# A scan's main loop: from a scheduler's order to a fixed source order, a tile of the next group's projections around each step of the mixing

## The chip, the cores and the metric

The kernel runs on one core of a Trainium2 chip, in one launch. The metric is the device time of one execution in microseconds (us). Five engines have a queue of instructions each and work through it in order: TensorE (PE: matmuls, with the loading of weights shown apart as PEld), VectorE (DVE), ScalarE (ACT), GpSimd (POOL) and SyncE (SP, which issues the DMA transfers). An instruction that waits for another engine holds up all that stand behind it in its own queue.

## The reference

The kernel computes a layer of three parts, each added to `x` (16 x 32 x 512): a graph attention over a context, a state-space scan, and a small gated feed-forward network. The change touches the scan alone. Cut to what matters (128 heads of 64 channels, 8 groups of 16 heads, 128 states; sequences of 32, so one chunk holds a whole sequence):

```python
proj = jnp.einsum('bsd,od->bso', h, in_proj_w)
gate = proj[..., :D_INNER]                       # D_INNER = 8192
hBC = jax.nn.silu(causal_conv(hBC, conv_w, conv_b))
hid, B, C = split(hBC)
dt = jax.nn.softplus(dt + dt_bias)
A = -jnp.exp(A_log)
L = jnp.exp(segsum(A * dt))                      # decay from one position to a later one
M = einsum('bcihn,bcjhn->bcijh', C, B) * L
y = einsum('bcijh,bcjhp->bcihp', M, hid * dt) + Dp * hid
yg = y * jax.nn.silu(gate)
ygr = yg * rsqrt(mean over a group of 1024 channels of yg**2 + EPS)
out = residual + (ygr * gnorm_w) @ out_proj_w.T
```

## The kernel before

The graph part takes the first 1300 us and more, the scan runs until 2276 us of the profiled execution, and the feed-forward part follows. All 512 tokens are four blocks of 128. In the scan, tokens lie along the free axis wherever channels lie on the partitions. The 8192 inner channels are 64 tiles of 128 channels, two heads each; eight tiles make a group.

Per tile `t` (group `g`, step `i`) the work is:

- `project` (L1177): the weights of a tile (256 KB, `win`, a ring of six buffers shared by the gate half `wing` and the current half `winch`) are loaded by SP (L1174) and four matmuls of 128x512 make a product in PSUM (`pp`, two buffers). For the gate half ACT makes `gs = silu(pp)` (L1256).
- `convolve` (L1184 to L1192): for the current half, ACT writes the product times the last tap plus bias (`cy`), DVE adds the three other taps (L1189, three instructions), ACT makes `hid = silu(cy)` (L1192).
- `mix`, once for each tile of a group: four transposes of `hid` on PE (`pht`, L1285), DVE multiplies by `dt` (`hd`, L1287), DVE multiplies decay by `CB` for either head (`el`, L1298, two instructions), eight matmuls give the tile's output in PSUM (`py`, L1306). DVE adds `Dp * hid` (L1310) and multiplies by the gate (`gs`, L1311). ACT squares (L1316), POOL adds the square to the group's sum `ssq` (L1317; the first tile's square is written to `ssq` by ACT, L1313), and ACT scales by `gnorm_w` (L1318).
- `decays`, once for a pair of tiles (four heads): POOL makes `da` (L1265), one 128x512 matmul makes its running sums (`pl`, L1270), ACT takes the exponential (`ed`, L1275). `da` and `ed` have two buffers each. `pl` and `pht` share two PSUM buffers (`ps_m`).
- `close`, once for a group: four small matmuls sum `ssq` over the channels (`pn`, L1325), DVE and ACT make the inverse root (`rstd`, seven instructions), SP loads the eight tiles of the output weights (`wo`, 256 KB each, a ring of ten, L1333), and for each of the four token blocks eight 128x512 matmuls (`po`, L1338, two PSUM buffers) are added to `xt` by DVE, times the root (L1341).

The source runs `inner(g + 1)` (all eight tiles' projections and convolutions of the next group), then `mix(g)`, then `close(g)`. But that isn't the order of the queues: in the scan a scheduler orders instructions by priority and by when their inputs and buffers come free, so that on PE the projections, transposes, `py`, `pl` and `po` of two groups stand mixed, `py` matmuls partly one by one between others. On POOL it puts `da` as early as a buffer is free.

`inner` also advances `parts` by one step for each tile from the second group on. `parts` is the loading of the feed-forward part's low-rank weights (`LowRank.load`): ten pieces, each with nine small loads on SP (L185) and eight DVE instructions (`split`, L167 to L173).

Of the kernel before, what the change touches and what calls it, by code (L numbers as in the profile page):

```python
# [8 lines left out]
F32 = mybir.dt.float32  # L9
# [3 lines left out]
AF = mybir.ActivationFunctionType  # L13
ALU = mybir.AluOpType
# [4 lines left out]
P = 128  # L19
B = 16  # L20
C = 32
D = 512
# [9 lines left out]
CB = 3  # L32
# [8 lines left out]
H_M, G_M, SEQ = 128, 8, 32  # L41
D_INNER = 8192
NT = D_INNER // P
TG = NT // G_M
# [9 lines left out]
def kernel(ctx: ExitStack, tc: tile.TileContext, I, out):  # L54
# [69 lines left out]
    with ExitStack() as cx:  # L124
        scan_part(nc, tc, cx, I, id32, ones, xt, U, rstd, lows)
# [4 lines left out]
class LowRank:  # L130
# [4 lines left out]
    def __init__(self, nc, tc, const, I):  # L135
        self.nc, self.tc, self.I = nc, tc, I
        self.weights = {
            n: const.tile([P, w], BF16, name=f"lb{n}") for n, w in (("1", HT * NHT), ("3", HT * NHT), ("2", D))
        }
        self.values = {n: const.tile([P, D], BF16, name=f"lv{n}") for n in ("1", "3", "2")}  # L140

        self.of = [const.tile([LR, 3], F32, name=f"lof{k}") for k in range(2)]
# [969 lines left out]
def scan_part(nc, tc, cx, I, id32, ones, xt, u, rstd, lows):  # L1112
# [3 lines left out]
    wk = cx.enter_context(tc.tile_pool(name="swk", bufs=2))  # L1116
    sm = cx.enter_context(tc.tile_pool(name="ssm", bufs=3))
    wpool = cx.enter_context(tc.tile_pool(name="sw", bufs=4))
    ps_p = cx.enter_context(tc.tile_pool(name="sps_p", bufs=2, space=PSUM))
    ps_m = cx.enter_context(tc.tile_pool(name="sps_m", bufs=2, space=PSUM))  # L1120
    ps_y = cx.enter_context(tc.tile_pool(name="sps_y", bufs=2, space=PSUM))
# [24 lines left out]
    for t, base, cmul, op, b2, c2, s2 in ((le, 0, -1, ALU.is_ge, 0, 1, -32), (gt, 0, 1, ALU.is_gt, 31, -1, 32)):  # L1146
        nc.gpsimd.memset(t, 1.0)
        nc.gpsimd.affine_select(
            out=t, in_=t, compare_op=op, fill=0.0, base=base, pattern=[[-cmul, P]], channel_multiplier=cmul
        )  # L1150
        nc.gpsimd.affine_select(
            out=t, in_=t, compare_op=ALU.is_ge, fill=0.0, base=b2, pattern=[[s2, 4], [0, 32]], channel_multiplier=c2
# [10 lines left out]
    for q in range(4):  # L1163
        pt = ps_m.tile([P, 4, P], F32, tag="m", name=f"pt{q}")
# [6 lines left out]
    def project(t, tag):  # L1171

        w = wpool.tile([P, 4, P], F32, tag="win", name=f"win{tag}", bufs=6)
        nc.sync.dma_start(out=w, in_=I["in_proj"][t])  # L1174
        pp = ps_p.tile([P, D], F32, tag="p", name=f"pp{tag}")
        for k in range(4):
            nc.tensor.matmul(pp, lhsT=w[:, k], rhs=hT[:, k], start=(k == 0), stop=(k == 3))  # L1177
        return pp

    def convolve(dst, t, tag):  # L1180

        pp = project(NT + t, f"c{tag}")
        y = wk.tile([P, B, SEQ], F32, tag="cy", name=f"cy{tag}", bufs=3)
        nc.scalar.activation(  # L1184
            y.rearrange("p b s -> p (b s)"), pp, AF.Identity, bias=cb[:, t:t + 1], scale=cw[:, t, 3:4]
        )
        pv = pp.rearrange("p (b s) -> p b s", b=B)
        for sh in (1, 2, 3):
            nc.vector.scalar_tensor_tensor(  # L1189
                y[:, :, sh:], pv[:, :, :SEQ - sh], cw[:, t, 3 - sh:4 - sh], y[:, :, sh:], ALU.mult, ALU.add  # L1190
            )
        nc.scalar.activation(dst, y.rearrange("p b s -> p (b s)"), AF.Silu)  # L1192


    wdt = wpool.tile([P, 4, P], F32, tag="win", name="wdt", bufs=6)
# [36 lines left out]
    CB = sc.tile([P, G_M, 4, P], F32, name="CB")  # L1232
# [13 lines left out]
    parts = lows.load(low)  # L1246
    big = cx.enter_context(tc.tile_pool(name="sbig", bufs=2))

    def inner(g):

        gs = big.tile([P, TG, D], F32, tag="gs", name=f"gs{g}")
        hid = big.tile([P, TG, D], F32, tag="hid", name=f"hid{g}")
        for i in range(TG):
            t = g * TG + i
            pg = project(t, f"g{t}")
            nc.scalar.activation(gs[:, i], pg, AF.Silu)  # L1256
            convolve(hid[:, i], t, f"h{t}")
            if g > 0:
                next(parts, None)
        return gs, hid  # L1260

    def decays(h):

        da = sm.tile([P, 4, 4, SEQ], F32, tag="da", name=f"da{h}", bufs=2)
        nc.gpsimd.tensor_tensor(  # L1265
            da, lei.unsqueeze(1).unsqueeze(1).to_broadcast([P, 4, 4, SEQ]),
            dA[:, :, h:h + 4].rearrange("p q h -> p h q").unsqueeze(3).to_broadcast([P, 4, 4, SEQ]), ALU.mult,
        )
        pl = ps_m.tile([P, 4, 4, SEQ], F32, tag="m", name=f"pl{h}")
        nc.tensor.matmul(  # L1270
            pl.rearrange("p h q i -> p (h q i)"), lhsT=gt, rhs=da.rearrange("p h q i -> p (h q i)"),
            start=True, stop=True,
        )
        ed = sm.tile([P, 4, 4, SEQ], F32, tag="ed", name=f"ed{h}", bufs=2)
        nc.scalar.activation(ed, pl, AF.Exp)  # L1275
        return ed

    def mix(g, gs, hid):

        ssq = wk.tile([P, D], F32, tag="ssq", name=f"ssq{g}")  # L1280
        for i in range(TG):
            t = g * TG + i
            pt = ps_m.tile([P, 4, P], F32, tag="m", name=f"pht{t}")
            for q in range(4):
                nc.tensor.transpose(pt[:, q], hid[:, i, q * P:(q + 1) * P], id32)  # L1285
            hd = sm.tile([P, 4, 2, 64], F32, tag="hd", name=f"hd{t}")
            nc.vector.tensor_tensor(  # L1287
                hd, pt.rearrange("p q (h c) -> p q h c", h=2),
                dt[:, :, 2 * t:2 * t + 2].unsqueeze(3).to_broadcast([P, 4, 2, 64]), ALU.mult,
            )  # L1290
            py = ps_y.tile([P, 4, P], F32, tag="y", name=f"py{t}")
            if i % 2 == 0:
                decay = decays(2 * t)
            els = []
            for j in range(2):

                el = sm.tile([P, 4, P], F32, tag="el", name=f"el{2 * t + j}")
                nc.vector.tensor_tensor(  # L1298
                    el.rearrange("p q (b i) -> p q b i", b=4),
                    decay[:, 2 * (i % 2) + j].unsqueeze(2).to_broadcast([P, 4, 4, SEQ]),  # L1300
                    CB[:, g].rearrange("p q (b i) -> p q b i", b=4), ALU.mult,
                )
                els.append(el)
            for q in range(4):
                for j in range(2):
                    nc.tensor.matmul(  # L1306
                        py[64 * j:64 * j + 64, q], lhsT=hd[:, q, j], rhs=els[j][:, q], start=True, stop=True
                    )
            pyf = py.rearrange("p q t -> p (q t)")
            nc.vector.scalar_tensor_tensor(hid[:, i], hid[:, i], dpc[:, t:t + 1], pyf, ALU.mult, ALU.add)  # L1310
            nc.vector.tensor_tensor(gs[:, i], gs[:, i], hid[:, i], ALU.mult)  # L1311
            if i == 0:
                nc.scalar.activation(ssq, gs[:, i], AF.Square)  # L1313
            else:
                sq = wk.tile([P, D], F32, tag="sq", name=f"sq{t}")
                nc.scalar.activation(sq, gs[:, i], AF.Square)  # L1316
                nc.gpsimd.tensor_tensor(ssq, ssq, sq, ALU.add)  # L1317
            nc.scalar.activation(gs[:, i], gs[:, i], AF.Copy, scale=gnw[:, t:t + 1])  # L1318
        return ssq

    def close(g, gs, ssq):

        pn = ps_y.tile([P, 4], F32, tag="y", name=f"pn{g}")
        for q in range(4):
            nc.tensor.matmul(pn[:, q:q + 1], lhsT=ssq[:, q * P:(q + 1) * P], rhs=ones[:, 0:1], start=True, stop=True)  # L1325
        mean = sm.tile([P, 4], F32, tag="gm", name=f"gm{g}")
        nc.vector.tensor_scalar(mean, pn, 1.0 / (TG * P), None, ALU.mult)
        rs = sm.tile([P, 4], F32, tag="gr", name=f"gr{g}")
        rstd(sm, rs, mean, 4, f"gn{g}")
        wo = []  # L1330
        for i in range(TG):
            w = wpool.tile([P, D], F32, tag="wo", name=f"wo{g}_{i}", bufs=TG + 2)
            nc.sync.dma_start(out=w, in_=I["out_proj"][g * TG + i])  # L1333
            wo.append(w)
        for q in range(4):
            po = ps_o.tile([P, D], F32, tag="o", name=f"po{g}_{q}")
            for i in range(TG):
                nc.tensor.matmul(  # L1338
                    po, lhsT=gs[:, i, q * P:(q + 1) * P], rhs=wo[i], start=(i == 0), stop=(i == TG - 1)
                )  # L1340
            nc.vector.scalar_tensor_tensor(xt[:, q], po, rs[:, q:q + 1], xt[:, q], ALU.mult, ALU.add)  # L1341

    cur = inner(0)
    for g in range(G_M):
        nxt = inner(g + 1) if g + 1 < G_M else None
        ssq = mix(g, *cur)
        close(g, cur[0], ssq)
        cur = nxt


def ffn_part(nc, tc, cx, I, id32, xt, layernorm, lows, out):
# [139 lines left out]
```

## Time and profile before

| what | us |
|---|---|
| median of 3 runs | 2381.26 (2378.29 to 2382.47) |
| the profiled execution's own time | 2376.64 |
| its span in the profile | 2374.9 |
| first gate projection of the scan's loop starts | 1424.3 |
| last `po` matmul of the loop ends, about | 2275.7 |
| PE busy over the span | 2172.0 (91%) |
| DVE, ACT, POOL busy over the span | 1694.5, 1093.6, 831.4 |

The profile comes from one execution. Its page cuts the span into 40 slices of 59.4 us; the scan's loop lies in slices 25 to 39. The groups of instructions carry the source line, the engine, the operation and the tile that they write and read, then how many there were, their busy time and mean duration, and what the engine waited for before them. A 128x512 matmul in f32 appears as two records. Matmuls overlap: a record lasts 0.59 us, but the next may start 0.43 us after it, so costs on PE are read from start to start. The granted clock of PE is given per stretch: 1.00 is full speed.

### The profile page before, as it was taken

How to read it: one execution, taken by the hardware profiler on the slowest of the kernel's cores; microseconds unless marked ns; L12 is line 12 of the kernel's file. 1: busy time of each engine (PE TensorE's matmuls, PEld its weight loads, DVE VectorE, ACT ScalarE, POOL GpSimd, SP SyncE). 2: the span in 40 equal slices, each digit the busy share in tenths (PEclk: the TensorE clock that was granted, in tenths of full speed). 3: DMA queues.
4: the chain of work that ended last, by engine and by line, in shares of the span. 5: the costliest groups of instructions: out<-in, count | busy, mean ns of one | idle time of the engine just before them, and what ended most of it. 6: DMA issues, size and time to landing. Idle time of an engine off the chain costs nothing. (4 is left out here: it accounts for less than half of the span.)

```text
span 2374.9 us, 88834 instructions
## 1 busy us (share of the span) xinstructions
PE 2172.0 (91%) x39234; PEld 1243.6 (52%) x39234; DVE 1694.5 (71%) x3674; ACT 1093.6 (46%) x2023; POOL 831.4 (35%) x897
## 2 busy tenths in 40 slices
PE   5598899999989988799999689999999999999979
PEld 2254555776547765477777444444444444444422
DVE  8487897998979999799899757455362635446543
ACT  6685666556755544355555233233242423333321
POOL 2155656556555566555555100021120202012200
PEclk9899999999999999999999799999999999999989
DMA  1323242231231412313111212212212031220000
GB/s 49 81 59 76 51 81 57 52 81 43 59 78 42 90 41 55 81 43 85 43 39 41 94 56 79 72 53 58 67 40 84 23 102 49 63 62 14 27 36 18
DMA packets 121625, 137.99 MB, mean 58 GB/s; under 512 B 18398, under 2 KB 79506, under 8 KB 121154
## 3 DMA queue, kind: packets, MB, share of 16 engines
q1 hardware_dynamic: 121240, 132.32, 22.6%
q8 instruction: 308, 5.05, 0.9%
q14 instruction: 77, 0.63, 0.1%
HBM read 77.02 MB, written 12.85 MB: 38 GB/s over the span
## 5 line engine op out<-in xcount | busy, mean ns | idle before, releaser
L888 POOL TENSOR_TENSOR EN<-e,rz 128x480 f32<-128x480 f32 x344 | 342.4, 995 | 509.6 <-DVE rz L886 423.1
L913 PE MATMUL u<-WA,DD 128*32 128x128 bf16 (+1 forms) x16512 | 412.5, 248 | 19.4 <-issue 19.1
L918 ACT COPY us<-u 128x512 f32<-128x512 f32 x516 | 301.9, 586 | 154.2 <-PE u L913 138.2
L913 PEld LDWEIGHTS <-DD 128*32 128x32 f16 x16512 | 337.5, 97 | 53.5 <-issue 51.1
L873 ACT ACTIVATE e<-s,smc 128x480 f32<-128x480 f32 x344 | 227.3, 661 | 270.2 <-PE s L868 243.5
L809 POOL TENSOR_TENSOR DD<-fs,crep 128x480 f16<-128x480 f32 (+2 forms) x344 | 349.4, 1016 | 0.0
L941 PE MATMUL h<-e,us 128*32 128x30 f32 (+1 forms) x11008 | 281.3, 210 | 47.1 <-DVE e L894 25.6
L941 PEld LDWEIGHTS h<-e,us 128*32 128x32 f32 (+1 forms) x11008 | 247.2, 125 | 147.0 <-issue 68.1
L1189 DVE SCALAR_TENSOR_TENSOR cyh<-ppch,t_conv_w,cyh 128x496 f32<-128x496 f32 (+2 forms) x192 | 137.5, 716 | 221.9 <-ACT cyh L1184 217.9
L860 DVE TENSOR_REDUCE c<-s 128x16 bf16<-128x480 f32 x344 | 220.0, 640 | 77.0 <-PE s L851 73.9
L1265 POOL TENSOR_TENSOR da<-lei,dA 128x512 f32<-128x512 f32 x32 | 40.6, 1269 | 612.6 <-PE pl L1270 577.6
L1338 PE MATMUL po<-wo,gs 128*128 128x512 f32 x512 | 240.5, 605 | 10.4 <-DVE xt L1341 10.3
L1177 PE MATMUL ppch<-hT,winch 128*128 128x512 f32 x512 | 232.2, 593 | 0.0
L1177 PE MATMUL ppg<-hT,wing 128*128 128x512 f32 x512 | 231.9, 593 | 0.0
L894 DVE STREAM_TRANSPOSE e<-EN 128x512 f32<-128x512 f32 x344 | 224.5, 653 | 0.0
L880 DVE TENSOR_REDUCE z<-e 128x16 f32<-128x480 f32 x344 | 219.4, 638 | 0.4 <-ACT e L873 0.4
L541 ACT ACTIVATE sgn<-kd 128x512 bf16<-128x512 f32 x256 | 153.1, 598 | 48.6 <-PE kd L540 45.7
L851 PEld LDWEIGHTS <-DD 128*32 128x32 f16 x5504 | 80.8, 96 | 156.8 <-issue 131.6
L751 DVE TENSOR_SCALAR oh<-it,rank 128x512 bf16<-128x512 f16 x512 | 156.6, 366 | 7.6 <-PE pp L705 7.5
L1177 PEld LDWEIGHTS ppch<-hT,winch 128*128 128x128 f32 x512 | 93.6, 190 | 122.7 <-issue 122.4
L851 PE MATMUL s<-DX,DD 128*32 128x120 f16 x5504 | 141.5, 222 | 16.9 <-DMA DX<-DD 15.7
L1177 PEld LDWEIGHTS ppg<-hT,wing 128*128 128x128 f32 x512 | 95.8, 190 | 114.0 <-issue 114.0
(327 smaller groups left out, 2845.5 us busy)
## 6 DMA issues: line engine op xcount, KB each, us to landing
DX<-DD SPq DMA_DIRECT2D x456, 90.0 KB
wo<-in_out_proj SPq DMA_DIRECT2D x64, 256.0 KB
wing<-in_in_proj SPq DMA_DIRECT2D x64, 256.0 KB
winch<-in_in_proj SPq DMA_DIRECT2D x64, 256.0 KB
crep<-dC SPq DMA_DIRECT2D x128, 64.0 KB
dS<-so SPq DMA_DIRECT2D x32, 256.0 KB
fs<-dS SPq DMA_DIRECT2D x128, 64.0 KB
wincB<-in_in_proj SPq DMA_DIRECT2D x8, 256.0 KB
```

The source lines that it names most:

```text
L809: nc.gpsimd.tensor_tensor(d[:, :, m0 - n0:n1 - n0], win, crep[:, :, m0:n1].unsqueeze(3).to_broadcast([P, 4, n1 - m0, K]), ALU.subtract,)
L851: nc.tensor.matmul(s[rh, j * 4 * QB:(j + 1) * 4 * QB].rearrange("p (b q) -> p b q", b=4), lhsT=d[:, h, c0:c0 + 32], rhs=dx[:, h, :, c0:c0 ...
L860: nc.vector.tensor_reduce(c, live["s", at, gi].rearrange("p (i q) -> p i q", q=QB), AX.X, ALU.max, negate=True)
L873: nc.scalar.activation(e, s.rearrange("p (i q) -> p i q", q=QB), AF.Exp, scale=smc)
L880: nc.vector.tensor_reduce(z, e, AX.X, ALU.add)
L888: nc.gpsimd.tensor_tensor(en[:, :, :QB], e, rz.unsqueeze(2).to_broadcast([P, NI, QB]), ALU.mult)
L894: nc.vector.transpose(e.rearrange("p i q -> p (i q)"), en.rearrange("p i q -> p (i q)"))
L913: nc.tensor.matmul(u[rh, jj], lhsT=d[:, h, c0:c0 + 32], rhs=WA[k][:, h].rearrange("p b o -> p (b o)"), start=(jj == 0 and k == 0), stop=(k ...
L918: nc.scalar.copy(us[:, j - jj:j + 1], u)
L941: nc.tensor.matmul(h[r:r + co, pr, q0:q0 + QB], lhsT=us[:, j, b * co:(b + 1) * co], rhs=e[:, 4 * j + b, :QB], start=npair > 1, stop=True, ...
L1177: nc.tensor.matmul(pp, lhsT=w[:, k], rhs=hT[:, k], start=(k == 0), stop=(k == 3))
L1338: nc.tensor.matmul(po, lhsT=gs[:, i, q * P:(q + 1) * P], rhs=wo[i], start=(i == 0), stop=(i == TG - 1))
```

## The change

Around the whole loop the scheduler is turned off (`manual_schedule`): every queue now holds its instructions in the order in which the source issues them. The source is reordered with it.

- The first group's projections and convolutions are issued tile by tile ahead of the loop, and the first pair's decays.
- In step `i` of group `g` the source issues: the gate projection of tile `i` of the next group with its Silu on ACT; the end of the convolution of the tile before (three DVE instructions, Silu); `gated(i - 1)` (DVE twice, square on ACT, `ssq` add on POOL, scaling on ACT); `turn(i)` (transposes; in odd steps the decays of the next pair: `da` on POOL, `pl` on PE, `ed` on ACT; then `hd` and both `el` on DVE, and the load of this tile's `wo`); the current projection of the next group's tile with the first ACT instruction of its convolution; `outputs(i)` (the eight `py` matmuls).
- After the eighth step the convolution ends, `gated(7)` follows, and the group is closed with 32 `po` matmuls in one piece, `pn` and the root after the first eight.
- The closing of the seventh group is spread over the steps of the eighth, which has no projections of a next group: four `po` matmuls a step.
- `parts` advances at the end of each convolution.
- The `hd` ring goes from three buffers to two (`el` keeps three, `ed` and `da` two).

The instructions themselves are the same. The diff, cut to its core:

```diff
-    def inner(g):
...
+    cx.enter_context(tc.manual_schedule())
+    made = {}
+
+    def gate(g, i):
+        if i == 0:
+            made[g] = [big.tile([P, TG, D], F32, tag=n, name=f"{n}{g}") for n in ("gs", "hid")]
+        pg = project(g * TG + i, f"g{g * TG + i}")
+        nc.scalar.activation(made[g][0][:, i], pg, AF.Silu)
+
+    def current(g, i):
+        t = g * TG + i
+        yield from convolve_steps(made[g][1][:, i], t, f"h{t}")
+        if g > 0:
+            next(parts, None)
...
+    def ahead(h):
+        if h < H_M:
+            decay[h] = decays(h)
...
+        def turn(self, i):
...
             for q in range(4):
-                nc.tensor.transpose(pt[:, q], hid[:, i, q * P:(q + 1) * P], id32)
-            hd = sm.tile([P, 4, 2, 64], F32, tag="hd", name=f"hd{t}")
+                nc.tensor.transpose(pt[:, q], self.hid[:, i, q * P:(q + 1) * P], id32)
+            if i % 2:
+                ahead(2 * t + 2)
+            hd = sm.tile([P, 4, 2, 64], F32, tag="hd", name=f"hd{t}", bufs=2)
...
-            py = ps_y.tile([P, 4, P], F32, tag="y", name=f"py{t}")
-            if i % 2 == 0:
-                decay = decays(2 * t)
...
+            w = wpool.tile([P, D], F32, tag="wo", name=f"wo{t}", bufs=TG + 2)
+            nc.sync.dma_start(out=w, in_=I["out_proj"][t])
+            self.wo.append(w)
...
+        def gated(self, i):
...
                 nc.scalar.activation(sq, gs[:, i], AF.Square)
                 nc.gpsimd.tensor_tensor(ssq, ssq, sq, ALU.add)
             nc.scalar.activation(gs[:, i], gs[:, i], AF.Copy, scale=gnw[:, t:t + 1])
...
-    cur = inner(0)
+    for i in range(TG):
+        gate(0, i)
+        end_of(current(0, i))
+    ahead(0)
+    last = None
     for g in range(G_M):
-        nxt = inner(g + 1) if g + 1 < G_M else None
-        ssq = mix(g, *cur)
-        close(g, cur[0], ssq)
-        cur = nxt
+        mix = Mix(g)
+        conv = None
+        for i in range(TG):
+            if g + 1 < G_M:
+                gate(g + 1, i)
+            end_of(conv)
+            conv = None
+            if i:
+                mix.gated(i - 1)
+            mix.turn(i)
+            if g + 1 < G_M:
+                conv = current(g + 1, i)
+                next(conv)
+            else:
+                next(last, None)
+            mix.outputs(i)
+        end_of(conv)
+        mix.gated(TG - 1)
+        end_of(last)
+        last = mix.closing()
+        if g + 2 != G_M:
+            end_of(last)
+            last = None
```

More of the change, by code (lines that the diff above doesn't have):

```diff
@@ L1178, in project, with convolve_steps @@
         return pp
-    def convolve(dst, t, tag):
+    def convolve_steps(dst, t, tag):
         pp = project(NT + t, f"c{tag}")
@@ L1186, in convolve @@
         )
+        yield
         pv = pp.rearrange("p (b s) -> p b s", b=B)
@@ L1192, in convolve @@
         nc.scalar.activation(dst, y.rearrange("p b s -> p (b s)"), AF.Silu)
+    def convolve(*args):
+        for _ in convolve_steps(*args):
+            pass
     wdt = wpool.tile([P, 4, P], F32, tag="win", name="wdt", bufs=6)
@@ L1247, in scan_part @@
     big = cx.enter_context(tc.tile_pool(name="sbig", bufs=2))
-    def inner(g):
[L1251 to L1260, printed above, removed]
+    cx.enter_context(tc.manual_schedule())
[10 more added lines that the diff above has]
+            next(parts, None)
     def decays(h):
@@ L1276, in decays, with __init__ @@
         return ed
[L1278 to L1282, printed above, removed]
+    decay = {}
+    def ahead(h):
+        if h < H_M:
+            decay[h] = decays(h)
+    class Mix:
+        def __init__(self, g):
+            self.g = g
+            self.gs, self.hid = made.pop(g)
+            self.ssq = wk.tile([P, D], F32, tag="ssq", name=f"ssq{g}")
+            self.wo = []
+            self.pairs = []
+            self.sums = None
+        def turn(self, i):
+            t = self.g * TG + i
             pt = ps_m.tile([P, 4, P], F32, tag="m", name=f"pht{t}")
             for q in range(4):
-                nc.tensor.transpose(pt[:, q], hid[:, i, q * P:(q + 1) * P], id32)
-            hd = sm.tile([P, 4, 2, 64], F32, tag="hd", name=f"hd{t}")
+                nc.tensor.transpose(pt[:, q], self.hid[:, i, q * P:(q + 1) * P], id32)
+            if i % 2:
+                ahead(2 * t + 2)
+            hd = sm.tile([P, 4, 2, 64], F32, tag="hd", name=f"hd{t}", bufs=2)
             nc.vector.tensor_tensor(
@@ L1290, in mix, with outputs @@
             )
-            py = ps_y.tile([P, 4, P], F32, tag="y", name=f"py{t}")
-            if i % 2 == 0:
-                decay = decays(2 * t)
             els = []
+            h0 = 4 * (t // 2)
             for j in range(2):
-                el = sm.tile([P, 4, P], F32, tag="el", name=f"el{2 * t + j}")
+                el = sm.tile([P, 4, P], F32, tag="el", name=f"el{2 * t + j}", bufs=3)
                 nc.vector.tensor_tensor(
                     el.rearrange("p q (b i) -> p q b i", b=4),
-                    decay[:, 2 * (i % 2) + j].unsqueeze(2).to_broadcast([P, 4, 4, SEQ]),
-                    CB[:, g].rearrange("p q (b i) -> p q b i", b=4), ALU.mult,
+                    decay[h0][:, 2 * (i % 2) + j].unsqueeze(2).to_broadcast([P, 4, 4, SEQ]),
+                    CB[:, self.g].rearrange("p q (b i) -> p q b i", b=4), ALU.mult,
                 )
                 els.append(el)
+            if i % 2:
+                decay.pop(h0)
+            self.now = hd, els
+            w = wpool.tile([P, D], F32, tag="wo", name=f"wo{t}", bufs=TG + 2)
+            nc.sync.dma_start(out=w, in_=I["out_proj"][t])
+            self.wo.append(w)
+        def outputs(self, i):
+            t = self.g * TG + i
+            hd, els = self.now
+            py = ps_y.tile([P, 4, P], F32, tag="y", name=f"py{t}")
             for q in range(4):
@@ L1308, in mix @@
                     )
-            pyf = py.rearrange("p q t -> p (q t)")
+            self.py = py
+        def gated(self, i):
+            t = self.g * TG + i
+            gs, hid, ssq = self.gs, self.hid, self.ssq
+            pyf = self.py.rearrange("p q t -> p (q t)")
             nc.vector.scalar_tensor_tensor(hid[:, i], hid[:, i], dpc[:, t:t + 1], pyf, ALU.mult, ALU.add)
@@ L1318, in mix, with closing, root @@
             nc.scalar.activation(gs[:, i], gs[:, i], AF.Copy, scale=gnw[:, t:t + 1])
-        return ssq
-    def close(g, gs, ssq):
+        def closing(self):
+            return close(self.g, self.gs, self.ssq, self.wo, self.pairs)
+    def root(g, ssq):
         pn = ps_y.tile([P, 4], F32, tag="y", name=f"pn{g}")
@@ L1329, in close @@
         rstd(sm, rs, mean, 4, f"gn{g}")
[L1330 to L1334, printed above, removed]
+        return rs
+    def close(g, gs, ssq, wo, pairs):
         for q in range(4):
@@ L1340, in close, with end_of @@
                 )
+                if i == TG // 2 - 1:
+                    yield
+            if q == 0:
+                rs = root(g, ssq)
             nc.vector.scalar_tensor_tensor(xt[:, q], po, rs[:, q:q + 1], xt[:, q], ALU.mult, ALU.add)
-    cur = inner(0)
-    for g in range(G_M):
-        nxt = inner(g + 1) if g + 1 < G_M else None
-        ssq = mix(g, *cur)
-        close(g, cur[0], ssq)
-        cur = nxt
+            yield
+    def end_of(c):
+        for _ in c or ():
+            pass
+    for i in range(TG):
[3 more added lines that the diff above has]
+    last = None
+    for g in range(G_M):
+        mix = Mix(g)
[21 more added lines that the diff above has]
+            last = None
 def ffn_part(nc, tc, cx, I, id32, xt, layernorm, lows, out):
```

## The prediction

> **What bounds the kernel now.** I read the page's slices first (PE is at 9 tenths from slice 25 to 36), then the busy time in stretches, to see whether PE is the bound of the scan's loop itself:
>
> ```profile
> 1760.00:1865.00 105.00, 103.76 (x369) 48.19 (x370) 50.40 (x76) 36.62 (x53) 14.84 (x12) 1.00 0.21 61
> ```
>
> The columns are the stretch, then busy us of PE, PEld, DVE, ACT and POOL, the granted clock and the DMA. One group takes 105 us (the pn matmuls start at 1572.9 in the first group and at 2202.0 in the seventh: 629.1 / 6 = 104.9), and PE is busy for 103.8 of it, at full clock. The other engines have half their time and more to spare. So PE's queue sets the time of the loop, and whatever makes PE wait is paid in full.
>
> Next the timeline, for what PE's pieces cost from start to start:
>
> ```profile
> 1439.02 3.60 PE L1177 MATMUL ppg<-hT,wing 128*128 128x512 f32 x8
> 1442.45 3.60 PE L1177 MATMUL ppch<-hT,winch 128*128 128x512 f32 x8
> ...
> 1641.94 1.09 PE L1306 MATMUL py<-el,hd 128*64 128x128 f32 x16
> 1642.97 1.09 PE L1285 MATMUL pht<-id,hid 128*128 128x128 f32 x8
> 1643.90 3.60 PE L1177 MATMUL ppg<-hT,wing 128*128 128x512 f32 x8
> ```
>
> A projection (four matmuls, eight records) takes 1442.45 - 1439.02 = 3.43 us, so a 128x512 matmul (two records) takes 0.86. A tile's py matmuls take 1.03, its four transposes 0.93 / 2 = 0.47. Last the groups by shape in 1420 to 2280 us, for the other engines' pieces (busy us, mean ns of one, then idle before and its releaser), and two rows of the waits:
>
> ```profile
> L1317 POOL TENSOR_TENSOR ssq<-ssq,sq 128x512 f32<-128x512 f32 x56 | 79.9, 1427 | 129.3 <-ACT sq L1316 129.2
> L1192 ACT ACTIVATE hid<-cyh 128x512 f32<-128x512 f32 x64 | 40.2, 628 | 125.1 <-DVE cyh L1189 125.1
> L1265 POOL TENSOR_TENSOR da<-lei,dA 128x512 f32<-128x512 f32 x30 | 38.5, 1282 | 577.9 <-PE pl L1270 577.6
> L1256 ACT ACTIVATE gs<-ppg 128x512 f32<-128x512 f32 x64 | 37.3, 583 | 94.8 <-PE po L1338 86.6 <-PE ppg L1177 6.7 <-PE pcb L1242 1.5
> L1316 ACT ACTIVATE sq<-gs 128x512 f32<-128x512 f32 x56 | 35.3, 630 | 95.2 <-DVE gs L1311 95.2
> ```
>
> ```profile
> POOL da L1265 <- PE pl L1270: 577.6, 22, 70.1
> PE po L1338 <- DVE xt L1341: 10.3, 8, 2.0
> ```
>
> The reader is to see that da now waits only for its buffer to come free: POOL makes it tens of us ahead, and no pl matmul ever waits for a da. That is what the change gives up.
>
> **The change, part by part.**
>
> *What the fixed order wins.* Per group PE has 16 projections (54.9), 32 po matmuls (27.5), 8 py (8.2), 8 pht (3.8), 4 pl (3.4) and pn (0.9): 98.7 of 104.9 us. The 6 us left are py matmuls scattered singly between others, and waits of po on xt. The new order issues py in one piece, and puts pn (which needs gated's last ssq) behind the first eight po, with the seven cheap steps of root beside the next 6.9 us of po. So I count PE's new time from its pieces. First group's projections 8 x 6.87 = 54.9 and a pl, 0.9. A tile of groups 0 to 6: 3.43 + 0.47 + 3.43 + 1.03 and 0.13 for two changes of matmul size = 8.49, x 56 = 475.4. 28 pl: 24.1. Closings of groups 0 to 5: 6 x 28.4 = 170.1. The last group, with the seventh's closing spread over it: 8 x 5.06, three pl and a pn = 44.0, and 4 for py waiting on el. Last closing with its xt 29.1. Sum 803. The same stretch of before (first gate projection at 1424.3 to the last xt, 2275.7 + 0.7) is 852. Without new waits the change would win 49.
>
> *What it adds: pl waits for POOL.* In odd steps the order on PE is gate projection, transposes, pl, current projection, py. On POOL da stands behind gated's ssq add of the tile before; on ACT that tile's square stands behind this step's gate Silu, which waits for this step's gate projection. Clock from the end of the previous py: gate projection done 3.43, transposes 3.97. ACT: 0.2 from PE to ACT (1641.42 + 0.43 to 1642.05 in the timeline), Silu 0.58, Silu of the current half 0.63, square 0.63: 5.5. DVE is no later (three conv steps, hid and gs: 3.6). POOL: 0.17, ssq 1.43, da 1.28: 8.4. PE may start pl at about 8.5, and has waited 8.5 - 4.0 = 4.5. Behind pl stand the current projection, py, and the next step's gate, so nothing fills the gap. Step 1 of a group has no ssq add to wait for, so its da is early. That leaves 3 stalls in each of seven groups; in the last (no projections, and no pl in step 7) 2 of 4.8, where DVE's hid and gs start the chain. 21 x 4.5 + 2 x 4.8 = 104. Bounds: POOL at its shortest here (1.26 and 1.05) 4.1 each, at its longest (1.75 and 1.63) 5.2.
>
> *What a stall costs besides.* PE's clock, in stretches of 3.4 us (us, PE busy, granted clock, DMA):
>
> ```profile
> 428.00:431.40 3.40, 1.39 (x31) 1.00 0.25 79
> 431.40:434.80 3.40, 3.40 (x62) 0.50 0.06 21
> 434.80:438.20 3.40, 3.40 (x114) 1.00 0.00 0
> ...
> 1373.50:1376.90 3.40, 0.92 (x8) 1.00 0.06 24
> 1376.90:1380.30 3.40, 1.91 (x3) 0.50 0.00 0
> 1380.30:1383.70 3.40, 3.40 (x12) 0.50 0.00 0
> 1383.70:1387.10 3.40, 3.40 (x9) 1.00 0.14 26
> ```
>
> A stretch busy for 40% or less is followed by half clock, until a stretch is busy throughout. A gap of 4.5 us puts at least 2.2 idle us into one such stretch, wherever it falls. Every gap of 3.9 us and more in this trace ended at half clock; of the eight between 2.0 and 2.6 us, two did. What it cost: PE worked at half clock for 5.3 us after the gap of 4.0 at 1374, 5.4 after 6.3 at 228, 5.4 after 6.0 at 686, 3.4 after 7.7 at 990. Half of their mean is 2.4 us. 23 x 2.4 = 55; bounds 0 and 23 x 3.3 = 76 (6.6 us at half each).
>
> The Trainium skill ("TensorE: Matmul & The Clock Gate", "What's actually happening") has the clock halve after at least one idle window of about 3.4 us. By that, only a gap that covers a whole window costs the clock, a third of those of 4.5 us, and the sum would be some 37 us lower, by estimate; the first row above (1.39 us busy, and still half clock after it) speaks against it.
>
> *LowRank's splits.* Ten steps of groups 0 and 1 have 3.4 us of DVE (8 instructions) put between conv and gated. DVE needs then some 9.9 us of an 8.5 us step, and py waits. I take 18 (1.8 a step); bounds 0 (as now, where DVE's other half hides them) and 25.
>
> *Moved at nothing.* wo loads go from the closing into each step, between wing and winch on SP, behind the wait for their slots: a slot's last reader is the closing before, by which time five win tiles are loaded ahead (17 us of projections); if that cover went, a step would wait up to the load's landing. The nine lw loads of a step take 9 x 0.3 us of SP's queue, within the step. In the last group wo loads wait for the closing's last quarter; two land beside the 5 us of po before them. ACT's extra table loads (1.28 each, about one a step) lie in its waits for PE. ed is made a step before it is read. FFN's loads still wait for the last xt.
>
> **Sum.** 803 + 104 + 55 + 18 = 980 against 852: 128 more. The profiled execution took 2376.6: 2505. The median of the runs is 4.7 higher than that execution; I say 2507.
>
> **Rivals.**
> - *Stalls without the loss of clock.* For it: gaps of 2 us mostly kept full clock. Against: all of 3.9 and more lost it. 2376.6 + 73 = 2450.
> - *The chain is shorter than I count, so that stalls are near 2.5 us and few lose the clock.* 803 + 18 + 58 + 15 - 852 = 42 more: 2419. For it: POOL and ACT are idle two thirds of the time. Against: the chain is serial, and its rows hardly vary.
> - *Faster: da is on time.* The place is POOL's queue: if da did not stand behind ssq, or the chain from the gate projection ended within the transposes, 803 + 18 - 852 = -31: 2346. It decides at a stall of 31 / 23 = 1.3 us, short enough to keep the clock; I count 4.5. For it: POOL is 86% idle and the decays are started a pair early. Against: the built order has ssq ahead of da, and pl ahead of the current projection, in every pair but a group's first.
> - *Worse: loads late.* Win tiles behind wo and lw on SP make PE wait in more steps: 2540 and up.
>
> **How the numbers follow.** Forecast 0.63, no clock loss 0.18, short stalls 0.07, worse 0.05, faster 0.05, near nothing 0.02. The range leaves out the last four: from 2440 (no clock loss, and POOL at its shortest, -9) to 2540 (clock loss at 76, +21, and POOL at its longest, +16, on 2505, rounded). About 0.2% is what a measurement of this kernel can tell from no change: faster 0.05, within 0.02, slower 0.93.
>
> **What would show it.** Right: PE's waits headed by pl on POOL's da, 23 of 4 to 5 us; PEclk at 7 or 8 tenths in slices 26 to 38; POOL's da waiting for ssq's square, no longer for pl; one group at 71.4 + 28.4 + 13.5 + 7.2 = 120 us; po's waits on xt gone. Wrong: no such wait, or full clock in the loop; then the first two terms, or the third, fall.

## The result and the profile after

The changed kernel takes 2506.95 us (2505.43 to 2511.32, 4 runs) against 2381.32 us before: ratio 1.0533, 95% interval 1.0514 to 1.0551. It is slower by 5.3%. The profiled execution has a span of 2505.5 us, 130.6 more than before, and nearly all of it arises in the scan's loop: from the first gate projection to the end of the last `po` matmul 2403.5 - 1422.2 = 981.3 us, against 2275.7 - 1424.3 = 851.4.

One group of the loop in stretches, as in the row shown of before (columns: stretch; busy us of PE, PEld, DVE, ACT, POOL; granted clock; DMA):

```profile
1838.90:1958.10 119.20, 106.80 (x369) 50.36 (x368) 47.13 (x74) 42.09 (x57) 15.22 (x12) 0.94 0.18 53
1958.10:2077.50 119.40, 107.01 (x371) 50.52 (x369) 47.13 (x74) 42.09 (x57) 15.57 (x12) 0.94 0.18 53
```

A group takes 119.3 us where it took 105, with the same matmuls. PE is idle for 12.4 us of it, and its mean clock is 0.94. The waits of PE in the loop (engine and line, who was waited for; us in total, times, longest):

```profile
PE pl L1277 <- POOL da L1272: 102.7, 25, 5.3
PE py L1339 <- DVE el L1320: 10.8, 12, 1.6
PE po L1377 <- ACT gs L1356: 1.9, 1, 1.9
```

All other waits of PE are gone, that of `po` on `xt` too. The one at the head is new: before, POOL waited for `pl`; now `pl` waits for POOL. The timeline of an odd step, all engines but PE's weight loads, shows the chain (start, us, engine, line):

```profile
1935.68 3.70 PE L1177 MATMUL ppg<-hT,wing 128*128 128x512 f32 x8
...
1938.49 0.69 DVE L1349 TENSOR_TENSOR gs<-gs,hid 128x512 f32<-128x512 f32 x1
1939.22 0.60 PE L1307 MATMUL pht<-id,hid 128*128 128x128 f32 x4
...
1939.42 0.60 ACT L1261 ACTIVATE gs<-ppg 128x512 f32<-128x512 f32 x1 [3.88 <-PE ppg L1177]
...
1939.91 0.62 ACT L1193 ACTIVATE hid<-cyh 128x512 f32<-128x512 f32 x1
1940.43 0.62 ACT L1354 ACTIVATE sq<-gs 128x512 f32<-128x512 f32 x1
1940.46 1.28 DVE L1320 TENSOR_TENSOR el<-ed,CB 128x512 f32<-128x512 f32 x2
...
1941.19 1.68 POOL L1355 TENSOR_TENSOR ssq<-ssq,sq 128x512 f32<-128x512 f32 x1 [6.85 <-ACT sq L1354]
...
1942.83 1.07 POOL L1272 TENSOR_TENSOR da<-lei,dA 128x512 f32<-128x512 f32 x1
1943.95 1.40 PE L1277 MATMUL pl<-da,gt 128*128 128x512 f32 x2 [4.13 <-POOL da L1272]
1945.15 5.06 PE L1177 MATMUL ppch<-hT,winch 128*128 128x512 f32 x8
1945.39 0.60 ACT L1282 ACTIVATE ed<-pl 128x512 f32<-128x512 f32 x1 [2.28 <-PE pl L1277]
1950.14 1.09 PE L1339 MATMUL py<-el,hd 128*64 128x128 f32 x16
```

ACT's Silu waits for this step's gate projection. Behind it, one after the other, come the second Silu, the square, POOL's ssq add and `da`, and PE stands 4.13 us before `pl`. Then the second cost is to be seen: the current projection takes 1950.14 - 1945.15 = 5.0 us in place of 3.4. The clock around it (stretch, PE busy, granted clock, DMA):

```profile
1941.20:1944.60 3.40, 0.65 (x2) 1.00 0.11 43
1944.60:1948.00 3.40, 3.40 (x6) 0.51 0.00 0
1948.00:1951.40 3.40, 3.40 (x22) 0.99 0.00 0
```

PE is at full clock while it idles, and at half clock in the 3.4 us after.

### The profile page after: what moved, and what is told of

Same layout as the page of the kernel before. It is cut to its first block, busy times and chain, and to the rows that moved or that the text cites. A ratio compares the mean times of both kernels' runs of the same rounds, so it can differ in the third digit from the quotient of the medians.

```text
span 2505.5 us, 88825 instructions
## 1 busy us (share of the span) xinstructions
PE 2205.8 (88%) x39234; PEld 1264.8 (50%) x39234; DVE 1678.0 (67%) x3674; ACT 1139.1 (45%) x2063; POOL 834.5 (33%) x897
## 5 line engine op out<-in xcount | busy, mean ns | idle before, releaser
L1355 POOL TENSOR_TENSOR ssq<-ssq,sq 128x512 f32<-128x512 f32 x56 | 88.6, 1582 | 761.8 <-ACT sq L1354 761.8
L1177 PE MATMUL ppch<-hT,winch 128*128 128x512 f32 x512 | 261.9, 659 | 0.0
L1177 PE MATMUL ppg<-hT,wing 128*128 128x512 f32 x512 | 238.0, 608 | 0.0
L1377 PE MATMUL po<-wo,gs 128*128 128x512 f32 x512 | 229.1, 604 | 1.9 <-ACT gs L1356 1.9
L1177 PEld LDWEIGHTS ppch<-hT,winch 128*128 128x128 f32 x512 | 108.3, 217 | 136.3 <-issue 134.9
L1261 ACT ACTIVATE gs<-ppg 128x512 f32<-128x512 f32 x64 | 38.1, 595 | 298.9 <-PE ppg L1177 297.4
L1377 PEld LDWEIGHTS po<-wo,gs 128*128 128x128 f32 x512 | 97.6, 194 | 120.5 <-issue 115.4
```

The costliest lines, as they stand in the source:

```text
L1377: nc.tensor.matmul(po, lhsT=gs[:, i, q * P:(q + 1) * P], rhs=wo[i], start=(i == 0), stop=(i == TG - 1))
```

## The experiments

All times stand beside runs of the kernel before on the same chip (2375.5 and 2374.0 us in the two sets), so ratios are compared. My theory was the prediction's: new waits of `pl` on a `da` that stands behind a chain, and half clock after each. The main rival was that the fixed order itself is the slower one, whatever POOL does.

**The waits alone: `da` one step earlier.** POOL's product is taken out of `decays` and issued in the even step before; `pl` stays where it is.

```diff
+    def product(h):
+        if h >= H_M:
+            return
         da = sm.tile([P, 4, 4, SEQ], F32, tag="da", name=f"da{h}", bufs=2)
...
+        das[h] = da
+
+    def decays(h):
+
+        da = das.pop(h)
...
             if i % 2:
                 decay.pop(h0)
+            else:
+                product(h0 + 4)
```

> POOL's da is issued in the even step before, one step ahead of its pl, and so stands ahead of the ssq add that it stood behind; PE's and ACT's order and all else stay. Theory (pl waits for a da that stands behind the chain gate projection, Silu, Silu, square, ssq add): the 103 us of pl's waits go, and with them the half clock in the loop, 2.4 us a stall; 2507 - 103 - 23 x 2.4 (or 60) = 2344 to 2349 us, granted clock 0.97 to 0.98 over the span. Rival A (the fixed order ties the engines step by step, and py's wait for el or a projection's wait for PSUM takes the place of pl's): little is won, 2440 us and up, with those waits heading the list. Rival B (the half clock comes of the order's other small gaps and not of the stalls): 2507 - 103 = 2404 us, clock still near 0.95.

Measured 2351.98 us, ratio 0.9902 (0.988 to 0.9925): 6.3 points less than the changed kernel, and faster than before. `pl` waits 0.5 us in the whole loop (first row), and a group takes 100.0 us with PE busy throughout at full clock (second row):

```profile
PE pl L1285 <- POOL da L1275: 0.5, 1, 0.5
```

```profile
1876.80:1976.80 100.00, 100.00 (x369) 48.19 (x368) 47.13 (x74) 42.11 (x57) 15.51 (x12) 1.00 0.20 64
```

The loop went from 981.3 to 826.3 us, 155 less, though the waits were 102.7. Most of the other 52 is the clock: in the changed kernel's loop PE works 109.0 us at half clock, here 13.6. At half clock its matmuls start 0.86 us apart and not 0.43, so half of the difference is lost, 48 us. Some 5 us are left that neither explains. Rival A and rival B both fall.

**The clock alone: fill the gap.** The wait stays, and PE is given useless work in it. The three matmuls go into the tile that `py` overwrites later.

```diff
+            self.py = ps_y.tile([P, 4, P], F32, tag="y", name=f"py{t}")
+            if i % 2 and i > 1 and 2 * t + 2 < H_M:
+                for _ in range(3):
+                    nc.tensor.matmul(
+                        self.py.rearrange("p q t -> p (q t)"), lhsT=id32, rhs=hT[:, 0], start=True, stop=True
+                    )
             if i % 2:
                 ahead(2 * t + 2)
...
```

> Three 128x512 matmuls (2.6 us) whose product is overwritten stand on PE between the transposes and pl in each step that stalls (odd steps from the fourth on); they start when PE would idle and end before da is there. Nothing else changes, so pl starts when it did. Theory (a stall costs the gap and besides it the clock, since the idle stretch halves it for work that comes after): the gap shrinks to some 1.5 us, the clock stays full in the loop, and the kernel with more work is faster by 23 x 2.4 to 23 x 2.9 us: 2440 to 2452 us. Rival (the half clock falls into time that PE waits anyway and costs nothing, or comes of something else): 2507 us, or more by what the filling delays.

Measured 2464.75 us, ratio 1.0372 (1.0354 to 1.0391): more work, and 1.6 points faster. I had expected 2440 to 2452; the gain is some 40 us and not 55 to 67. The odd step of this kernel on PE:

```profile
1922.29 0.60 PE L1307 MATMUL pht<-id,hid 128*128 128x128 f32 x4
1922.72 2.74 PE L1311 MATMUL py<-hT,id 128*128 128x512 f32 x6
1927.02 1.12 PE L1277 MATMUL pl<-da,gt 128*128 128x512 f32 x2 [1.56 <-POOL da L1272]
1927.98 2.31 PE L1177 MATMUL ppch<-hT,winch 128*128 128x512 f32 x5
```

`pl` starts as late after the transposes as before (1927.02 - 1922.29 = 4.7; in the changed kernel 1943.95 - 1939.22 = 4.7). The gap is 1.56 us, and the same group at full clock takes 113.2 us in place of 119.3:

```profile
1826.30:1939.50 113.20, 108.53 (x387) 51.35 (x386) 47.13 (x74) 42.10 (x57) 15.19 (x12) 1.00 0.18 56
```

So three stalls of a group cost 6.1 us by the clock, 2.0 each, on top of the gaps.

**The same with transposes.** 24 transposes in place of the three matmuls:

```diff
...
+                for _ in range(6):
+                    for q in range(4):
+                        nc.tensor.transpose(self.py[:, q], self.hid[:, i, q * P:(q + 1) * P], id32)
...
```

> As the filling with three matmuls, but with 24 transposes of 128x128 (2.8 us of PE by the profile) whose output is overwritten. If the clock goes by PE's being at work of any kind, it is as fast as with matmuls: 113 us a group, 2460 to 2465 us. If transposes don't count as work, the clock halves as in the changed kernel, 119 us a group and 2500 us or more. The Trainium skill (TensorE: Matmul & The Clock Gate, on transposes) says that transpose mode doesn't count as busy the same way; no gap of the runs so far shows it.

Measured 2462.27 us, ratio 1.0371 (1.0354 to 1.0389): the same as with matmuls, and full clock in the group:

```profile
1822.70:1935.90 113.20, 108.64 (x442) 56.11 (x441) 47.11 (x74) 42.12 (x57) 15.19 (x12) 1.00 0.17 56
```

**The chain: one link out.** On ACT the gate's Silu goes behind the square and the scaling, so that the square no longer waits for this step's gate projection. No other queue changes.

```diff
...
-        pg = project(g * TG + i, f"g{g * TG + i}")
-        nc.scalar.activation(made[g][0][:, i], pg, AF.Silu)
+        made[g][2][i] = project(g * TG + i, f"g{g * TG + i}")
+
+    def silu(g, i):
+        nc.scalar.activation(made[g][0][:, i], made[g][2][i], AF.Silu)
...
                 mix.gated(i - 1)
+            if g + 1 < G_M:
+                silu(g + 1, i)
             mix.turn(i)
```

> On ACT the gate's Silu goes behind gated's square and scaling; no other queue changes. Theory (the chain before da is gate projection, Silu, Silu, square, ssq, da): the square then waits only for DVE's gs, which in the changed kernel ends 3.5 us after py; square 0.6, ssq 1.7, da 1.1 and 0.3 between engines end at 7.2 in place of 8.3, so each of the 21 stalls beside projections falls from 4.1 to about 3.0 us: 24 us less by the gaps alone, and up to 44 more where the shorter gap keeps the clock: 2440 to 2483 us. Rival (ssq starts when it does for another reason, POOL's own or a wait on PE, and ACT's order is no part of it): stalls stay at 4.1, 2500 us and up.

Measured 2478.39 us, ratio 1.0432 (1.0416 to 1.0448). The gaps of the second to seventh group fell to 3.0 us (2.5 to 3.3), as the chain says; those of the first group (4.0 to 5.3) and the last (4.3 and 4.8) did not:

```profile
1929.38 0.63 ACT L1356 ACTIVATE sq<-gs 128x512 f32<-128x512 f32 x1 [0.75 <-DVE gs L1351]
...
1930.16 1.26 POOL L1357 TENSOR_TENSOR ssq<-ssq,sq 128x512 f32<-128x512 f32 x1 [6.30 <-ACT sq L1356]
...
1930.57 2.88 DVE L1322 TENSOR_TENSOR el<-ed,CB 128x512 f32<-128x512 f32 x2
...
1931.38 1.52 POOL L1274 TENSOR_TENSOR da<-lei,dA 128x512 f32<-128x512 f32 x1
1932.95 1.13 PE L1279 MATMUL pl<-da,gt 128*128 128x512 f32 x2 [3.03 <-POOL da L1274]
```

The square now waits for DVE. The clock still fell after 13 of those 18 gaps, so the time lies in the upper half of what was expected.

**The low-rank pieces out of the steps.** They advance in the closings, where DVE has little to do.

```diff
-        if g > 0:
-            next(parts, None)
...
             nc.vector.scalar_tensor_tensor(xt[:, q], po, rs[:, q:q + 1], xt[:, q], ALU.mult, ALU.add)
+            next(parts, None)
             yield
```

> The low-rank weights' pieces advance in the closings (one after each token block) and no longer in the steps. Theory (DVE needs more than a step's 8.5 us where a split of 3.4 us stands in it, py and pl wait): py's and po's waits on el and gs in the first two groups (10.7 us), the longer stalls there (2 x 1.15) and the first group's extra pl stall (4.0, da behind the masks that wait for DVE) go, some 17 us and a little clock: 2485 to 2492 us. Rival (DVE has half its time idle, the split is hidden and the waits of the first groups are start-up): 2505 us or more, the closing's xt being late instead.

Measured 2492.15 us, ratio 1.05 (1.0469 to 1.053). The four runs lie 15 us apart, two at 2483 and 2487 and two at 2497 and 2498, and the interval overlaps that of the changed kernel: by the time alone this settles nothing. In the profile, which is of the fastest of the four, the loop is 20.5 us shorter (960.8). `py` waits 3.4 us in place of 10.8. `pl` waits 96.3 in place of 102.7: the first group's stall of 4.04 us is gone, and its two of 5.28 are 4.13 like the others. A new wait of 3.7 us is that of projections on their weights, behind the small loads on SP. To settle it, both edits were put together:

> da a step earlier and the low-rank pieces in the closings, both at once. Theory (stalls and splits are the two costs of the new order, and add up): the loop loses e1's remaining 14 us of the first groups as well: 2330 to 2340 us, group periods of 100 us from the first on. Rival (the splits only move the wait): as with da alone, 2348 to 2356 us.

Measured 2337.07 us, ratio 0.9842 (0.9828 to 0.9857), clear of 0.9902 with `da` alone. The splits cost 0.6 of a point, some 14 us, and the two costs add up. The first two intervals from `pn` to `pn` are 102.2 us, where 100 was expected from the first on, and the next three 100.0.

**The fixed order alone: the scheduler left on.** One line is taken out of the changed source, `cx.enter_context(tc.manual_schedule())`.

> The changed source with the scheduler left on. On PE the order is that of the changed kernel but for some eleven places; on POOL every da stands one pair earlier; on ACT and DVE the order of a step differs, and wo loads and splits are issued earlier. Theory (what costs is da's place on POOL and not PE's fixed order): no pl wait, 2335 to 2350 us, faster than the kernel before. Rival A (PE's order with a tile of projections around each step is itself worse than the mixed one): 2440 us and up.

Measured 2330.12 us, ratio 0.9808 (0.9789 to 0.9827), the fastest of all, 1.9% below the kernel before. PE's order is that of the changed kernel but for a few places, and the scheduler, which was in force, lets POOL run a pair ahead. POOL again waits for `pl`, and no more the other way round:

```profile
POOL da L1271 <- PE pl L1276: 292.3, 30, 39.8
```

```profile
1859.00:1959.00 100.00, 100.00 (x369) 48.19 (x368) 47.19 (x74) 42.51 (x58) 15.86 (x11) 1.00 0.21 64
```

This kernel differs from the changed one on ACT, DVE and SP too, so it doesn't isolate POOL as the first experiment does. But it shows that the new order of PE is the better one: 100.0 us a group against 105, PE never idle in between.

## Why the prediction was right

The forecast was 2507 us, and 2506.95 was measured. That close a hit has luck in it. The sum gave 2505 for the profiled execution, which took 2507.39, and of the 4.7 us named for the median only 2 were added. The terms were off by up to some 10 us, in both directions.

| term of the sum | forecast | measured | from |
|---|---|---|---|
| the loop without new waits | 803 | 814 | `da` early and splits in the closings: 813.4, and the last `xt` |
| the same under the scheduler | | 804 | scheduler left on: 1422.7 to 2226.2, and the last `xt` |
| `pl` waiting for `da` | 104 in 23 | 102.7 in 25 | waits of the changed kernel |
| half clock after the stalls | 55 | 44 to 48 | filling, 981.3 - 937.2; work at half clock after the 24 long gaps, 96 us / 2 |
| low-rank splits | 18 | 13 to 20 | with `da` early 826.3 - 813.4; alone 981.3 - 960.8 |

- *What bounds the kernel* held: PE's queue does. Taking PE's waits away shortened the loop by all of them, and by the clock besides.
- *What the fixed order wins* held: `py` in one piece and no wait of `po` on `xt`. A group takes 100.0 us at best; I had 99.8 (71.4 and 28.4). But the whole loop comes to 814 and not 803 when the two costs are out: the first two intervals from `pn` to `pn` are 2.2 us longer each than 100.0, and from the sixth closing's `pn` to the eighth's it takes 152.0 us, where the scheduler's kernel needs 145.5.
- *pl waits for POOL* held in its mechanism, place and size: one chain, three stalls a group, and none above 0.5 us in step 1 of groups 2 to 8. A single stall is 4.13 and not 4.5 us; two of the first group, where the splits stand in the steps, are 5.28. ACT's three instructions start 0.5 us apart, closer than their durations of 0.6; `da` took 1.07 where I had its mean of before, 1.28, and ssq 1.67 where I had 1.43. One stall was not forecast: 4.04 us in step 1 of the first group. There `da` stands behind the low-rank masks and 4.3 us of memsets, and a mask's memset waits for a DVE copy that stands behind the convolution.
- *What a stall costs besides* was mis-sized: 2.0 us and not 2.4. All 24 gaps of 4 us and more were followed by half clock (at one, in the last group, it had begun before the gap). But after 14 of them it lasted one stretch of 3.4 us, which began about when work did; I had taken the mean of four gaps, all followed by two stretches or more. The reading that every gap of 3.9 us and more ended at half clock in the trace of before holds from 66 us on, where its record of the clock starts; behind a gap of 4.3 us at 47.4 us the view has 1.00.
- *LowRank's splits*: right in size, if what they add to the stalls of the first group is counted with them.
- *Moved at nothing*: held for `wo`, the table loads and `ed`. PE waited for no load in the changed kernel's loop.
- One sign was wrong: the page's clock in slices 26 to 38 is 9 tenths in ten and 8 in three, not 7 or 8. The sum itself had said as much: 55 us lost means 110 us at half clock in 980, a mean of 0.94.
- The rival "stalls without the loss of clock" is what the filling made, `pl` starting as late and the clock kept: 2465, where I had 2450. The rival "da is on time" would have come to 2346; the kernel that has `da` early runs at 2352.

The change lost because one instruction on a nearly idle engine was issued in the same step as the matmul that needs it, behind an instruction that waits for that step. What it meant to do, it does: with `da` early the same order beats the kernel before by 1%.

What stays open: the 5 us of the 155 won by the early `da` that are neither waits nor half clock. That the last full interval from `pn` to `pn` takes 105.0 us in that kernel has a plain reason: from the last `py` of the seventh group to its `pn` it takes 11.9 us (2169.9 to 2181.8) where the group before has 7.0, because two `pht`, a `py`, a `pl` and 1.3 us of waits of the eighth group stand in between.

## What to carry to other kernels

Before an order is fixed by hand, write down for each engine what stands ahead of each instruction in its queue; "a pair ahead" in the data is worth nothing if the producer is issued behind an instruction that waits for this step. A producer on an idle engine belongs a step earlier, ahead of everything in its queue that waits for the bounding engine. And a gap of some us on PE can cost more than its length: the gaps of 4 us here half as much again.

## What the runs showed of the hardware

- Half clock followed 24 of 24 gaps of 4.0 us and more in the changed kernel, 13 of 18 gaps of 2.5 to 3.3 us with the Silu moved, and none of 19 gaps of 1.6 us with the matmuls filled in. Short gaps are not safe for that: in the changed kernel half clock also followed three spots (about 1511, 1593 and 1644 us) where PE stood for 1.5, 1.9 and 2.8 us in one or two pieces, and with the filling one of two gaps of 2.7 us.
- The Trainium skill ("TensorE: Matmul & The Clock Gate", "What's actually happening") speaks of at least one idle window of about 3.4 us. Gaps of 3.0 us can't hold such a window, and still most were followed by half clock. The granted clock changes on a grid of 3.41 us in these traces. Cut on it, the changed kernel's loop has 25 stretches at full clock in which PE was busy for 41% or less, and half clock followed each; of 16 that were busy for 47 to 66% it followed two (55 and 58%). So a stretch that is busy for some 40% was enough here, and what decides above that stays open.
- Work whose result is thrown away, put into the gaps while the waits stayed, made the kernel 1.6 points faster.
- Transposes kept the clock at full speed as well as matmuls did (113.2 us a group with either). The same page ("Part 4: PE-mode transpose") says that they don't count as busy in the same way; 24 transposes of 128x128 in f32 in each gap were enough here.
- When POOL's ssq and `da` ran beside DVE's two el products (the step with the Silu moved, shown above), these took 2.88 us together, where the changed kernel's timeline has 1.28. In that run an el beside which POOL did nothing took 0.67 to 0.69 us (34 of 128), and one that had POOL at work beside it for most of its time 1.40 on average (85). DVE's busy time of the group shown rises from 47.1 to 55.7 us with the same 74 instructions:

```profile
1831.97:1947.13 115.16, 105.52 (x369) 49.92 (x368) 55.68 (x74) 42.53 (x57) 15.42 (x12) 0.96 0.17 55
```
